# The sixth output pair's rows turned by VectorE instead of TensorE

## The chip, the cores and the metric

The kernel runs on one core of a Trainium2 chip. The time is the device time of one execution in microseconds (us), from start to end on that core. Profiles are of one execution, taken by the hardware profiler; in them PE is TensorE's matmul, PEld its weight load, DVE is VectorE, ACT ScalarE, POOL GpSimd and SP SyncE; a trailing q (SPq, ACTq) marks the queue that issues DMAs.

## The reference

One layer of masked attention over a graph of 2708 nodes with 1024 features, all in float32:

```python
h = jnp.maximum(_layernorm(x, axis=-1), 0.0)
q = h @ W_q.T + b_q;  k = h @ W_k.T + b_k;  v = h @ W_v.T + b_v
z = (1 / sqrt(1024)) * (q @ k.T)
spare_z = z * adj
spare_z = where(spare_z == 0.0, -10000.0, spare_z)
out = x + relu(softmax(spare_z, axis=1) @ v)
```

`adj` is 0 or 1 with a chance of 0.0014771 for a 1, so a row has about four neighbours.

## The kernel before

**What it computes.** Since rows have few neighbours, nothing dense of size 2708 x 2708 is formed. The kernel builds M = W_q^T W_k once, finds the neighbours of each row, sorts the rows by their number of neighbours and cuts them into tiles of 128 rows. For a tile t, K[t] is the largest number of neighbours in it. Sorted tiles with few neighbours have few slots: K is 3 for tile 18, 5 for 12, 2 for 19, 6 for 11, 4 for 15, 6 for 10, 4 for 14, 7 for 1, 4 for 16, 7 for 9 and 8 for 8. Then, for each tile:

- q = h M + b (a matmul with 1024 x 1024), stored to `q_dram` or `q_late`;
- **scores**: for each slot s, POOL gathers the neighbours' rows of h into a buffer `g` (L610, an indirect DMA), and one DVE instruction multiplies them with `pq`, the tile's q loaded back by SP (L833), and sums the products (L863);
- **weights**: an exponential on ACT, a few tiny DVE instructions (L906 to L911), and u = coef0 * g0 on ACT (L912);
- **sums**: for each further slot one DVE instruction u += coef * g (L923);
- out = x + relu(u W_v^T + b_v): another matmul with 1024 x 1024, then an indirect DMA that adds x (L1110) and one that scatters the rows (L808).

**Units.** Both matmuls are done for two tiles at a time, a *unit*, as a Strassen-Winograd product of 2 x 2 blocks with seven block products instead of eight. Units 0 to 9 form q (`q_pairs`), units 10 to 19 the output (`o_pairs`, in the order of `order`): 10 is (6, 5), 11 (4, 3), 12 (2, 0), 13 (20, 7), 14 (17, 13), 15 (18, 12), 16 (19, 11), 17 (15, 10), 18 (14, 1), 19 (16, 9). The sixth output pair is unit 15. Tile 8 is left over (`alone`) and done at the very end.

`multiply(n, results, after)` writes the seven products of unit n and calls `after(0)` to `after(6)` between them. In `after(i)` everything else is placed: `now` is [n, i], called step (n, i) here. The operands of unit n + 1 are made in unit n: `ops_of[n + 1][1]()` (upper) at i = 0 and `[2]()` (lower) at i = 2. Rows of unit n + 2 are loaded at i = 4 by `load_rows`.

**Turning.** A matmul needs the rows turned (features on partitions). `blocks(xa, xb)` has two ways for the rows of a tile:

- by TensorE: `half_turned` (L415) issues four 128 x 128 transposes for each half of a tile into PSUM. ACT copies three of a pair's four halves out (`held`, L718); DVE reads the fourth, a21, straight from PSUM for s1 and s3 (L722);
- by VectorE, for a tile that is *faced*: VectorE turns 32 x 32 blocks, so the blocks must already lie in the right partitions. When u is finished, ACT copies it into a tile `v` with its columns reordered (L945) and stores that (L947); `by_quarters` (L700) loads it back with four DMAs of 128 KB, each for 32 partitions, with 256 floats a piece; `faces` (L705) is one DVE transpose of 128 x 512 for each half. s3 is then formed in place (L742).

**Which way, and the generator.** All DVE work of the attention is one Python generator, `attention`, that yields a charge for each instruction: 1.3 for a score or a sum, 0.6 for weights. `advance(share)` in each `after` lets it go on until the charges reach `share`:

```python
share = (20.9 if n < len(units) - 5 else 21.5) / 7
if nxt is not None and nxt[0] == "o":
    share -= 2.3 / 7 * len(set(nxt[1:]) & faced_tiles)
```

so a unit that prepares a unit with faced tiles gets less of the stream. When the last sum of a tile t is issued, `sums(t)` decides by `now` and t's unit: faced (into `faced_tiles`); or, if `near(t)` (the unit is at most two ahead), *held*: u stays in its row buffer and becomes the rows of its unit without a store; or stored by SP (L951) and loaded by SP as a whole (L1212). Before the change, units 10 to 14 are faced, unit 19 and tile 8 too (`unit >= len(units) - 1`); of the others, 18, 12, 19 and 15 are stored and loaded, and 11, 10, 14 and 1 are held. If the tiles of unit n + 2 are not done when it loads, `advance(1.0)` is repeated until they are.

DVE runs in the order of the program (`manual_schedule`); the other engines' orders are the scheduler's. SP's queue also carries the loads of `pq` (two buffers), the store of one row for the tail (`tail_dram`, L1130) and its load (L1183). Row tiles (u, v and loaded rows) rotate through seven buffers. For tile 8, `faces` makes `T_alone` in unit 19, and the product `ps<-M,T_alone` uses it; after that come the last products and the final adds of x.

Of the kernel before, what the change touches and what calls it, by code (L numbers as in the profile page):

```python
# [65 lines left out]
def tile_preln_masked_attention(  # L66
# [144 lines left out]
    def row_tile(name):  # L211
        return work.tile([P, D], FT, tag="row", name=name, bufs=ROWS)
# [626 lines left out]
    def fill():  # L839
        while wanted and free:  # L840
            t, s = wanted.pop(0)
            g = free.pop(0)
            if s == K[t]:
                half = slice(HOSTS.index(t) * HP, (HOSTS.index(t) + 1) * HP)
                nc.gpsimd.dma_start(g[:HP], v_dram[half, :])
            else:
                with tc.issue_after(first_q[0].ins) if first_q else nullcontext():
                    gathered.append(gather(g, h_dram[:, :], t, s, P, skip=True))
            g_of[t].append(g)

    def chained(step):

        with tc.issue_after(chain[-1].ins):
            chain.append(step())
# [64 lines left out]
    def sums(t):  # L919
        u, coef, m = us.pop(t)  # L920
        for s in range(0 if t in EMPTY else 1, K[t]):
            fill()
            chained(lambda: nc.vector.scalar_tensor_tensor(  # L923
                u, g_of[t][s], coef[:, s:s + 1], u, op0=ALU.mult, op1=ALU.add))
            free.append(g_of[t][s])
            yield 1.3
        fill()
        if t in HOSTS:
            chained(lambda: nc.vector.scalar_tensor_tensor(
                u[:HP], g_of[t][K[t]][:HP], m[:HP, 3:4], u[:HP], op0=ALU.mult, op1=ALU.add))  # L930
            free.append(g_of[t][K[t]])
            yield 1.3
            fill()
        g_of.pop(t)
        if t == SECOND:
            nc.sync.dma_start(v_dram, u)
            whole_second.append(True)
            return
        unit = next((n for n, pair in enumerate(units) if pair[0] == "o" and t in pair[1:]), len(units))
        if now < [unit - 2, 2] and unit <= len(q_pairs) + 4 or unit >= len(units) - 1:  # L940
            faced_tiles.add(t)
        print("done", t, "at", now, "unit", unit, t in faced_tiles)
        if t in faced_tiles:
            v = row_tile(f"v_{t}")
            nc.scalar.copy(v.rearrange("p (a c r) -> p c a r", a=QUADS, r=QP),  # L945
                           u.rearrange("p (c a r) -> p c a r", a=QUADS, r=QP))
            nc.scalar.dma_start(u_dram[t * P:(t + 1) * P, :], v)  # L947
        elif near(t):
            held[t] = u
        else:  # L950
            nc.sync.dma_start(u_dram[t * P:(t + 1) * P, :], u)  # L951
        done.add(t)
# [7 lines left out]
    def attention(order):  # L960
        for t in order[:2]:
            ask(t)
        free.extend(slots)

        fetch(order[0])
        fill()
        yield 0.0
        marked(0, EARLY)
        yield 0.0
        after = order[1:] + [None, None]  # L970
        yield from scores(order[0], after[0])
        for i, t in enumerate(order):
            nxt = after[i]
            ahead = nxt is not None and K[t] + K[nxt] <= HIGH + 1
            part = scores(nxt, after[i + 1]) if nxt is not None else iter(())
            if ahead:

                for _ in range(min(2, K[nxt] - 1)):
                    yield next(part, 0.0)
            weights(t)  # L980
            yield 0.6
            if ahead:
                yield from part
            yield from sums(t)
            yield from part
# [8 lines left out]
    spent, now = [0.0], [0, 0]  # L994

    def near(t):

        return t == alone or any(t in unit[1:] for unit in units[:now[0] + 3] if unit[0] == "o")
# [193 lines left out]
    q_pairs = [(t, t + 1) for t in range(0, BARE, 2)]  # L1192
    o_pairs = [(order[i], order[i + 1]) for i in range(0, FULL - 1, 2)]
    alone = order[-1]
    units = [("q",) + p for p in q_pairs] + [("o",) + p for p in o_pairs]
# [367 lines left out]
```

## Time and profile before

| | |
|---|---|
| time, median of 3 runs | 638.43 us (636.95 to 638.96) |
| the profiled execution | 638.0 us, span 636.3 us |
| mean granted TensorE clock | 0.995 |
| busy: ACT, POOL | 283.5 us (45%), 361.8 us (57%) |
| moved by DMA | 180.11 MB, 283 GB/s on average |
| stores of faced tiles, `u_dram<-v` (ACT's queue) | 13 of 512 KB |
| loads by quarters, `or<-u_dram` | 52 of 128 KB |
| other stores and loads of u (SP) | 4 and 4 of 512 KB |

The span is from the first to the last instruction of the profile; the execution's own time is 1.7 us more. All times within the profile count from the start of the span. In the lines of groups and of the timeline, `out<-in` are the program's names, followed by the operand shapes and the count; what stands in brackets is the idle time of the engine just before and what ended it. In a timeline, equal neighbours are merged into one line with their count. The chain is the work that ended last, followed back from the last instruction.

### The profile page before, as it was taken

The numbers are of one execution on the slowest core, as the hardware profiler recorded it, in microseconds if no ns is written. First come the engines' busy times: TensorE is split into PE (matmuls) and PEld (weight loads), VectorE is DVE, ScalarE is ACT, GpSimd is POOL, SyncE is SP. The second block draws the span as 40 slices with busy tenths as digits, with TensorE's granted clock in tenths as the row PEclk, the third lists the DMA queues.
The fourth block names the chain that finished last, engine by engine and source line by source line (L and its number), as shares of the span: only waits on it lengthen the run. The fifth ranks groups of instructions, "written<-read, shape, count | busy, mean of one in ns | idle before, by whom it ended". The sixth has DMA issues, their size and how long they took to land.

```text
span 636.3 us, 6139 instructions
## 1 busy us (share of the span) xinstructions
PE 624.6 (98%) x1627; PEld 315.5 (50%) x1627; DVE 525.7 (83%) x1021; ACT 283.5 (45%) x421; POOL 361.8 (57%) x383
## 2 busy tenths in 40 slices
PE   9999999999999999999999999999999999999994
PEld 5777766444444544444444434444444444444441
DVE  5999889897995755997889999999999989898341
ACT  3539975859667533424341243443343333422300
POOL 2649960975868277563742563576566777632431
PEclk9999999999999999999999999999999999999997
DMA  8998897598696439986699998999999999893761
GB/s 339 407 372 310 334 351 298 199 342 328 246 382 221 170 113 334 326 299 196 194 289 323 297 412 216 311 318 324 351 378 321 334 299 295 242 289 95 210 217 40
DMA packets 62352, 180.11 MB, mean 283 GB/s; under 512 B 10039, under 2 KB 17031, under 8 KB 61672
## 3 DMA queue, kind: packets, MB, share of 16 engines
q0 software_dynamic: 25136, 78.41, 39.4%
q1 hardware_dynamic: 31242, 80.19, 35.8%
q10 hardware_dynamic: 5934, 21.06, 8.5%
q8 instruction: 15, 0.25, 0.2%
q14 instruction: 25, 0.20, 0.1%
HBM read 147.23 MB, written 42.31 MB: 298 GB/s over the span
## 4 chain that ended last, share of the span: by engine, by line
PE 85%; DVE 6%; issue 4%; DMA 3%; SPq 1%; POOL 0%; ACT 0%; POOLq 0%; DVEq 0%; ACTq 0%
PE ps L1011 38%; PE psy L1011 28%; PE ps_y L476 6%; PE ps_x L476 4%; PE ps_z L476 4%; PE pt L415 3%; DVE u L923 2%; DMA g<-h_dram,tab 1%; DMA or<-u_dram 1%; DVE junk L863 1%; DVE s L722 1%; DVE wlow L1270 1%; PE ps_y L511 1%; SPq L700 1%; DVE q L1092 0%
## 5 line engine op out<-in xcount | busy, mean ns | idle before, releaser
L610 POOL DMA_INDIRECT g<-h_dram,tab x94 | 121.4, 1291 | 84.4 <-DVE u L923 31.1
L1011 PE MATMUL ps<-M,a 128*128 128x512 f32 x320 | 144.0, 593 | 0.0
L1011 PE MATMUL psy<-wlow,s 128*128 128x512 f32 x320 | 143.9, 592 | 0.0
L863 DVE SCALAR_TENSOR_TENSOR junk<-g,pq 128x1024 uint8<-128x1024 f32 x93 | 113.7, 1222 | 14.0 <-DMA g<-h_dram,tab 10.9
L1011 PEld LDWEIGHTS ps<-M,a 128*128 128x128 f32 x320 | 59.8, 190 | 70.8 <-issue 70.6
L1011 PEld LDWEIGHTS psy<-wlow,s 128*128 128x128 f32 x320 | 59.7, 190 | 70.2 <-issue 69.4
L923 DVE SCALAR_TENSOR_TENSOR u<-g,coef,u 128x1024 f32<-128x1024 f32 x69 | 88.4, 1281 | 6.9 <-ACT u L912 5.8
L389 DVE FIND_INDEX8 at<-ones,adj 128x8 uint32<-128x685 f32 (+1 forms) x88 | 74.5, 865 | 0.0
L1011 PE MATMUL psy<-wlow,a 128*128 128x512 f32 x160 | 72.0, 593 | 1.4 <-DVE q L1092 1.4
L1011 PE MATMUL ps<-M,s 128*128 128x512 f32 x160 | 72.1, 592 | 0.0
L1011 PE MATMUL ps<-wlow,s 128*128 128x512 f32 x160 | 72.0, 593 | 0.1
L368 ACT ACTIVATE sized<-adj 128x2708 uint8<-128x2708 f32 (+1 forms) x22 | 54.3, 2468 | 7.5 <-DMA adj<-in_adj_dram 6.2
L298 POOL TENSOR_TENSOR hsum<-hsum,x 128x256 f32<-128x256 f32 (+1 forms) x56 | 38.7, 729 | 25.6 <-DVE wlow L444 21.2
L1110 POOL DMA_INDIRECT y<-in_x_dram,tab x19 | 34.8, 1832 | 29.1 <-ACT y L1127 15.9
L1011 PEld LDWEIGHTS psy<-wlow,a 128*128 128x128 f32 x160 | 30.3, 190 | 40.0 <-issue 37.1
L1011 PEld LDWEIGHTS ps<-wlow,s 128*128 128x128 f32 x160 | 30.3, 190 | 38.6 <-issue 37.9
L1011 PEld LDWEIGHTS ps<-M,s 128*128 128x128 f32 x160 | 30.3, 190 | 38.1 <-issue 37.4
L912 ACT ACTIVATE u<-g,coef 128x1024 f32<-128x1024 f32 x18 | 20.7, 1147 | 32.1 <-DVE coef L911 32.1
L808 POOL DMA_INDIRECT out_dram<-y,tab x21 | 25.0, 1188 | 16.4 <-DVE flag L1354 6.1
L626 POOL DMA_INDIRECT tab_dram<-tab,pos_i x22 | 21.9, 995 | 20.7 <-DVE pos_i L689 15.3
L276 ACT ACTIVATE x<-x,r 128x1024 f32<-128x1024 f32 (+1 forms) x22 | 25.9, 1235 | 7.3 <-POOL r L266 7.3
L760 ACT COPY ps<-bp_sb 128x512 f32<-128x512 f32 x42 | 24.5, 595 | 7.2 <-DVE y L1145 6.7
(251 smaller groups left out, 843.5 us busy)
## 6 DMA issues: line engine op xcount, KB each, us to landing
adj<-in_adj_dram SPq DMA_DIRECT2D x21, 1354.0 KB, 11.3
x<-in_x_dram SPq DMA_DIRECT2D x21, 512.0 KB, 3.9
h_dram<-x ACTq DMA_DIRECT2D x21, 512.0 KB, 8.7
u_dram<-v ACTq DMA_DIRECT2D x13, 512.0 KB, 6.4
or<-u_dram SPq DMA_DIRECT2D x52, 128.0 KB, 7.0
q_late<-q SPq DMA_DIRECT2D x12, 512.0 KB, 6.0
pq<-q_late SPq DMA_DIRECT2D x12, 512.0 KB, 8.6
M<-in_wv_dram SPq DMA_DIRECT2D x4, 1024.0 KB
```

The costliest lines, as they stand in the source:

```text
L276: nc.scalar.activation(xs[i][:n], xs[i][:n], AF.Relu, bias=r[:n, 4, i:i + 1], scale=r[:n, 3, i:i + 1])
L298: small.append(nc.gpsimd.tensor_add(hsum[:n, cols], hsum[:n, cols], xt[:n, cols]))
L368: nc.scalar.activation(sized[:n], a[:n, :, :PW], AF.Abs, accum_out=total[:n, t:t + 1])
L389: nc.vector.max_index(at[:n, k - first_k, g, :], ones[:n, 0:8], a[:n, g, :])
L476: mm = nc.tensor.matmul(bank, a_tile(o + H * a[0], a[1], i), b(o), start=first and o == 0, stop=(o == H - 1), skip_group_check=True)
L610: return nc.gpsimd.indirect_dma_start(out=dst, out_offset=None, in_=src, in_offset=off, bounds_check=N - 1, oob_is_err=False)
L760: nc.scalar.copy(return_[h], row[:, h * NB:(h + 1) * NB])
L808: to = nc.gpsimd.indirect_dma_start(out=out, out_offset=bass.IndirectOffsetOnAxis(ap=ptab.bitcast(U32)[:n, t, SLOTS:SLOTS + 1], axis=0), i ...
L863: chained(lambda: nc.vector.scalar_tensor_tensor(junk, g_of[t][s], 1.0, tq[t], op0=ALU.mult, op1=ALU.mult, accum_out=zall[:, t, s:s + 1]))
L923: chained(lambda: nc.vector.scalar_tensor_tensor(u, g_of[t][s], coef[:, s:s + 1], u, op0=ALU.mult, op1=ALU.add))
L1011: mm = nc.tensor.matmul(bank, a[:, c, :], b[:, c, :], start=False, stop=(c == 3), skip_group_check=True)
L1110: return nc.gpsimd.indirect_dma_start(out=y[:n], out_offset=None, in_=x, in_offset=off, compute_op=ALU.add)
```

## The change

The bound on the units whose tiles are faced goes up by one:

```diff
         unit = next((n for n, pair in enumerate(units) if pair[0] == "o" and t in pair[1:]), len(units))
-        if now < [unit - 2, 2] and unit <= len(q_pairs) + 4 or unit >= len(units) - 1:
+        if now < [unit - 2, 2] and unit <= len(q_pairs) + 5 or unit >= len(units) - 1:
             faced_tiles.add(t)
```

`len(q_pairs)` is 10, so unit 15, tiles 18 and 12, comes under the rule, if each of them is done before step (13, 2). For a faced tile the rest follows from code that is unchanged: ACT copies u to v and stores it, SP loads it by quarters, DVE turns it, and the share of the stream in unit 14 is reduced.

## The prediction

> **What bounds the kernel now.** I read the page first, its busy shares and its chain:
>
> ```profile
> PE 624.6 (98%) x1627; PEld 315.5 (50%) x1627; DVE 525.7 (83%) x1021; ACT 283.5 (45%) x421; POOL 361.8 (57%) x383
> DVE  5999889897995755997889999999999989898341
> PE 85%; DVE 6%; issue 4%; DMA 3%; SPq 1%; POOL 0%; ACT 0%; POOLq 0%; DVEq 0%; ACTq 0%
> ```
>
> PE is busy for 98% of the span, and VectorE (DVE) is nearly full just before the end. Next, the chain in order of time (start, length, what), where the two groups of transposes of unit 15 stand, and three lines of PE's timeline (start, busy time, instruction, count), the products that need s1 of unit 15 and T_alone among them:
>
> ```profile
> 468.94 0.87 PE pt L415 x8
> ...
> 473.25 0.87 PE pt L415 x8
> ```
> ```profile
> 487.70 3.60 PE L1011 MATMUL ps<-wlow,s 128*128 128x512 f32 x8
> ...
> 494.57 1.04 PE L415 MATMUL pt<-ident,or 128*128 128x128 f32 x8
> ...
> 609.69 3.60 PE L1011 MATMUL ps<-M,T_alone 128*128 128x512 f32 x8
> ```
>
> The chain runs through PE alone in the output stages up to the last few us, and PE's lines show no idle time there, so the end moves exactly as PE's instruction list does, until something on another engine makes PE wait. Two things can do that: the operands s1 to s4 of a pair, and T_alone, the turned rows of tile 8, for which the whole DVE stream must be over. The second is the tight one, in DVE's timeline:
>
> ```profile
> 468.41 2.61 DVE L923 SCALAR_TENSOR_TENSOR u<-M,coef,u 128x1024 f32<-128x1024 f32 x2
> 470.94 1.24 DVE L863 SCALAR_TENSOR_TENSOR junk<-g,pq 128x1024 uint8<-128x1024 f32 x1
> ...
> 591.14 1.27 DVE L929 SCALAR_TENSOR_TENSOR u<-g,m,u 64x1024 f32<-64x1024 f32 x1
> ...
> 605.03 1.25 DVE L705 STREAM_TRANSPOSE T_alone<-or 128x1024 f32<-128x1024 f32 x1 [11.56 <-DMA or<-u_dram]
> ```
>
> The stream ends at 591.14 + 1.27 = 592.41. A copy, a store and four loads later T_alone is made, ready at 606.28. PE needs it at 609.69. That is 3.41 us of cover today.
>
> **Does the edit act?** The charges of the generator (1.3 a score or sum, 0.6 a weight step, against the share of each step) give tile 18 finished at step (12, 2) and tile 12 at (12, 6). Both lie before (13, 2) and belong to unit 15 = 10 + 5, so both become faced. Nothing before them changes. In unit 14 the share falls by 2 x 2.3/7 a step, from 2.99 to 2.33, 4.6 in the seven steps. By the same charges tile 15 then ends at (15, 0) instead of (14, 5) and is held, not stored and reloaded; tile 1 would be late, and three or four stream steps are forced at (16, 4), which brings the lag back; tile 8 is recorded as done at (18, 6) instead of (18, 5).
>
> **PE.** Sixteen transposes of unit 15 go, two groups of eight at 0.87 each in the chain: 2 x 0.87 = 1.74 us, all on the path. This is also the most that the change can bring.
>
> **ACT.** Three copies out of PSUM go; two copies u to v (1.05 us each) and two store issues come, at about 430 and 443, when u_18 and u_12 are done. They fall into idle time:
>
> ```profile
> 435.88 1.15 ACT L912 ACTIVATE u<-g,coef 128x1024 f32<-128x1024 f32 x1 [5.34 <-DVE coef L911]
> ...
> 446.21 1.15 ACT L912 ACTIVATE u<-g,coef 128x1024 f32<-128x1024 f32 x1 [4.11 <-DVE coef L911]
> ...
> 592.44 1.05 ACT L945 COPY v<-u 128x1024 f32<-128x1024 f32 x1 [0.55 <-DVE u L929]
> ```
>
> Cost nothing; without the idle time it would be 2.1 us on an engine that is 45% busy.
>
> **DVE's work.** Four transposes of 128x512 come. The sums s1 and s3 read SBUF instead of PSUM (0.69 against 0.64 each: 0.1 together). Unit 14 shows the price, and how a lower half waits for its loads:
>
> ```profile
> 447.23 1.30 DVE L705 STREAM_TRANSPOSE a<-or 128x512 f32<-128x512 f32 x2
> 448.45 1.18 DVE L863 SCALAR_TENSOR_TENSOR junk<-g,pq 128x1024 uint8<-128x1024 f32 x1
> ...
> 452.68 0.71 DVE L705 STREAM_TRANSPOSE a<-or 128x512 f32<-128x512 f32 x1 [0.49 <-DMA or<-u_dram]
> 453.31 0.67 DVE L705 STREAM_TRANSPOSE s<-or 128x512 f32<-128x512 f32 x1
> 454.09 0.69 DVE L722 TENSOR_TENSOR s<-a,s 128x512 f32<-128x512 f32 x1
> ```
>
> From start to next start that is 1.22 + 1.41 = 2.63, with the sums 2.7 us. DVE's idle time in the stretch that matters is in brackets here (the line at 488.11 is the first score of tile 14, for later), and the queue's answer has the landing time of a gather:
>
> ```profile
> 476.19 1.28 DVE L722 TENSOR_TENSOR s<-a,pt 128x512 f32<-128x512 f32 x2 [1.04 <-ACT a L718]
> 480.77 1.23 DVE L863 SCALAR_TENSOR_TENSOR junk<-g,pq 128x1024 uint8<-128x1024 f32 x1 [0.82 <-DMA g<-h_dram,tab]
> 488.11 1.22 DVE L863 SCALAR_TENSOR_TENSOR junk<-g,pq 128x1024 uint8<-128x1024 f32 x1
> 500.99 1.23 DVE L863 SCALAR_TENSOR_TENSOR junk<-g,pq 128x1024 uint8<-128x1024 f32 x1 [0.96 <-DMA g<-h_dram,tab]
> 510.87 0.69 DVE L1122 TENSOR_TENSOR p<-taken,p 128x512 f32<-128x512 f32 x1 [0.28 <-ACT taken L1076]
> 523.78 1.22 DVE L863 SCALAR_TENSOR_TENSOR junk<-M,pq 128x1024 uint8<-128x1024 f32 x1 [1.83 <-DMA M<-h_dram,tab]
> ```
> ```profile
> g<-h_dram,tab POOLq DMA_INDIRECT x94, 7.8
> ```
>
> The 1.04 goes, since it waited for an ACT copy that no longer exists: net 2.7 - 1.04 = 1.66. The other four, 3.89 together, wait for transfers and for PE; a DVE that runs late finds these ready, as long as the gathers do not move with it. Bounds for what they give back: 0 and 3.89. I take all 3.89, because a gather is on its way 7.8 us (median) before it is used, and a DVE that runs some us late meets it landed.
>
> **The new wait.** DVE must now wait for quarter loads of u_18 and u_12. SP, the tile's landing times in unit 14 (430 to 445) and the store just ahead of unit 15's loads (445 to 460):
>
> ```profile
> 430.49 7.86 SPq L700 DMA_DIRECT2D or<-u_dram  x8
> ...
> 460.85 0.80 SPq L1212 DMA_DIRECT2D or<-u_dram  x2
> 464.56 0.32 SPq L833 DMA_DIRECT2D pq<-q_late  x1
> 464.93 0.36 SPq L1183 DMA_DIRECT2D y<-tail_dram  x1
> 465.35 0.41 SPq L1212 DMA_DIRECT2D or<-u_dram  x1
> ```
> ```profile
> L951 SPq DMA_DIRECT2D u_dram<-u x2: 320/329/338, 430.1 to 443.2; - x2
> DMA to landing us min/median/max: 7.9/13.0/14.5
> ```
> ```profile
> L951 SPq DMA_DIRECT2D u_dram<-u x1: 320/320/320, 458.1 to 458.1; - x1
> DMA to landing us min/median/max: 6.6/6.6/6.6
> ```
> ```profile
> 430.00:438.00 8.00, 8.00 (x20) 3.54 (x19) 7.76 (x17) 2.64 (x5) 3.68 (x3) 1.00 1.04 349
> 461.00:467.00 6.00, 6.00 (x15) 2.66 (x14) 5.86 (x11) 2.65 (x5) 2.60 (x2) 1.00 1.03 414
> ```
>
> In unit 14 the store ahead landed at 430.1 + 7.9 = 438.0 and the last quarter 14.5 later, at 452.5, as DVE's wait up to 452.68 says. The DMA engines were full (share 1.04), as they are at 461 to 467 (1.03). For unit 15 the store of u_19 is ahead and lands at 458.1 + 6.6 = 464.7, so the last quarter is due at 464.7 + 14.5 = 479.2. DVE reaches the upper half after the first of the two sums at 468.41, at 469.72. With its two transposes (1.22) and one sum and two scores (3.8) it would be at the lower half at 474.7. It loses 479.2 - 474.7 = 4.5 us, part of it already at the upper half, since the first tile's quarters are due halfway, at about 472. Bounds: nothing, if they land as in unit 12 (rival two), and 8.5 (rival one). Behind these waits in DVE's queue stand the scores of tile 10 and the results of unit 14; PE needs s1 of unit 15 at 487.70 - 1.74 = 485.96 and gets it at 479.2 + 1.41 + 0.69 = 481.3, so no PE wait here. On SP the loads of pq_14, of the tail rows and of tile 19 stand behind the quarters; the first is wanted by the score at 488.11, the last by PE's transposes at 494.57. The nearest has 8.8 us after the last quarter, so that costs nothing. The two copies v take two more of the seven row buffers for some us, as they do in the units before, and I cost that at nothing; if a buffer comes late, the quarters do, which is rival one.
>
> [...]
>
> **Sum.** The end of the stream moves by 1.66 + 4.5 - 3.89 = 2.27 (its later waits for ACT, after a weight step, stay as they are). The round trip from there to T_alone stays: copy, store, loads. PE comes 1.74 earlier, so the cover is 609.69 - 1.74 - 606.28 = 1.67, and PE waits 2.27 - 1.67 = 0.6. The profiled execution took 638.0: 638.0 - 1.74 + 0.6 = 636.9. That execution lies 0.43 below the median of the runs, 638.43, so the forecast is 637.3.
>
> **Rivals.**
>
> One, slower: the quarters come so late that DVE hands its delay to PE at T_alone. The place is the lower half of unit 15. If the eight issues are drawn out as in unit 14 (7.86 from 460.85, to 468.7) and the last lands 14.5 after that, at 483.2, DVE loses 8.5, the stream ends 6.3 late, PE waits 4.6: 640.9, or 641.3 on the median. It decides from a last landing of 480.3 on (PE's wait is then 1.74); each us more costs one. Gathers that move with DVE, so that the 3.89 is not given back, work the same way. For it: loads that are issued 9 us before they are wanted, where unit 14 had 17 and still waited. Against it: less traffic ahead than in unit 14, and tile 15 saves 1 MB later on.
>
> Two, the cover holds: the quarters land as those of unit 12, for which the tile's answer between 372 and 400 has this:
>
> ```profile
> L700 SPq DMA_DIRECT2D or<-u_dram x8: 303/394/432, 388.1 to 392.6; - x8
> DMA to landing us min/median/max: 4.8/5.1/5.4
> ```
>
> Then DVE hardly waits, its 1.66 vanishes in the idle time, and the whole 1.74 stays: 636.3, 636.7 on the median. Against it: the DMA engines are full at 461.
>
> Three, the edit does nothing because a tile is done too late: 638.4. The room of three steps from (12, 6) to (13, 2), in code that the change leaves alone up to there, speaks against it.
>
> **Numbers.** Forecast 0.39, rival one 0.31, two 0.27, three 0.03. The runs before spread from 636.95 to 638.96, 0.3%; that is about what a measurement of this kernel can tell from no change, 1.9 us. The largest gain, 1.74, is just under it: half of rival two and a third of the forecast would measure as faster (0.27), all of rival one as slower (0.31), the rest as the same (0.42). The range goes from 635.9 (rival two less 0.8 of spread) to 641.3 (rival one's price); what lies outside is gathers that move along.
>
> **What would show it.** Sixteen transposes fewer at L415 and four more at L705; or<-u_dram by quarters 60 times, whole once; u_dram<-u once. Right, if DVE's wait for or<-u_dram in unit 15 is 3 to 6 us and PE's only new wait is under 1.5 us, at T_alone. Wrong, if PE waits at s1 of any pair, if DVE's later waits for gathers stay at 3.89, or if T_alone is ready before 607.9 or after 610.

## The result and the profile after

The change is slower, by half a percent: 641.85 us median (637.24 to 643.71) against 638.18 us (636.95 to 640.85) for the kernel before on the same chip, a ratio of 1.0051, 95% interval 1.004 to 1.0062. The forecast was 637.3 us, at most 641.3. Of the 22 executions of the change, five took 637.24 to 639.24 us and seventeen 640.75 to 643.71. The profiled one took 643.71 us (span 642.0), the longest, so the sizes below are those of a bad run; a milder one comes with the experiments. The ratios below compare with the kernel before on each experiment's own chip, since chips differ (its medians there lie between 637.8 and 639.9).

The two lines of the page, busy shares and chain:

```profile
PE 623.2 (97%) x1611; PEld 313.4 (49%) x1611; DVE 528.1 (82%) x1025; ACT 283.1 (44%) x420; POOL 364.6 (57%) x383
PE 58%; issue 13%; DMA 13%; DVE 9%; POOL 5%; ACT 1%; POOLq 0%; DVEq 0%; SPq 0%; ACTq 0%
```

PE has 16 instructions fewer and DVE four more, as the edit says. But the chain, 85% PE before, now leaves PE for long stretches. PE's timeline (start, busy time, what, and in brackets the idle time ahead and its releaser) has three waits between 425 us and the end, where the kernel before had none:

```profile
493.51 3.70 PE L1011 MATMUL psy<-wlow,a 128*128 128x512 f32 x8 [3.04 <-ACT taken L1076]
614.10 3.70 PE L1011 MATMUL ps<-M,T_alone 128*128 128x512 f32 x8 [1.77 <-DVE T_alone L705]
618.45 3.70 PE L1011 MATMUL psy<-wlow,a 128*128 128x512 f32 x8 [0.65 <-DVE p L1151]
```

DVE's timeline, the waits and the end of the stream:

```profile
477.59 1.30 DVE L705 STREAM_TRANSPOSE a<-or 128x512 f32<-128x512 f32 x2 [6.58 <-DMA pq<-q_late]
...
484.54 0.71 DVE L705 STREAM_TRANSPOSE a<-or 128x512 f32<-128x512 f32 x1 [2.07 <-DMA or<-u_dram]
...
491.63 0.69 DVE L1126 TENSOR_TENSOR u<-ps,u 128x512 f32<-128x512 f32 x1
...
531.59 1.23 DVE L863 SCALAR_TENSOR_TENSOR junk<-g,pq 128x1024 uint8<-128x1024 f32 x1 [1.00 <-DMA g<-h_dram,tab]
...
560.44 2.61 DVE L923 SCALAR_TENSOR_TENSOR u<-g,coef,u 128x1024 f32<-128x1024 f32 x2 [1.61 <-ACT u L912]
...
585.08 3.92 DVE L923 SCALAR_TENSOR_TENSOR u<-g,coef,u 128x1024 f32<-128x1024 f32 x3 [1.22 <-ACT u L912]
...
599.21 1.28 DVE L929 SCALAR_TENSOR_TENSOR u<-g,m,u 64x1024 f32<-64x1024 f32 x1
...
612.80 1.25 DVE L705 STREAM_TRANSPOSE T_alone<-or 128x1024 f32<-128x1024 f32 x1 [11.25 <-DMA or<-u_dram]
```

The third wait of PE follows from the second: DVE makes that `p` behind T_alone. The two waits of DVE in unit 14 for the loads by quarters come to 6.58 + 2.07 = 8.65 us. (The first row names `pq` as the releaser, but the instruction reads only `or`, and SP issued the load of `pq` behind the quarters; a releaser in brackets is an inference.) SP, and the tile's landing times:

```profile
459.44 0.32 SPq L951 DMA_DIRECT2D u_dram<-u  x1
461.85 0.25 SPq L1130 DMA_DIRECT2D tail_dram<-y  x1
462.17 4.87 SPq L700 DMA_DIRECT2D or<-u_dram  x8
469.68 0.34 SPq L833 DMA_DIRECT2D pq<-q_late  x1
```
```profile
L700 SPq DMA_DIRECT2D or<-u_dram x8: 303/430/577, 462.2 to 466.6; - x8
...
DMA to landing us min/median/max: 12.2/15.1/16.7
```

What joins DVE's wait to PE's first one is ACT, whose rows come in the order of its list:

```profile
489.34 1.15 ACT L912 ACTIVATE u<-g,coef 128x1024 f32<-128x1024 f32 x1 [7.54 <-DVE coef L911]
492.35 0.63 ACT L1127 ACTIVATE y<-u 128x512 f32<-128x512 f32 x1 [1.86 <-DVE u L1126]
492.89 0.57 ACT L1076 COPY taken<-psy 128x512 f32<-128x512 f32 x1
```

The copy `taken` empties the PSUM bank that PE adds a22 of unit 14 to next. It needs nothing from DVE. But in ACT's list it stands behind a weight step (489.34) and behind `y<-u`, which waits for DVE's add at 491.63, and both come late because in DVE's list their sources stand behind the loads by quarters. So the wait for unit 15's rows stops a product of unit 14.

The account fits. Without its waits PE would reach T_alone at 614.10 - 1.77 - 3.04 = 609.29; the forecast had 609.69 - 1.74 = 607.95. So this run is 1.34 us late beside its bracketed waits. PE is 0.92 of that late ahead of the edit's place (the product that started at 465.35 before starts at 466.27), and the rest is that the waits delay PE's next starts by 0.2 to 0.3 us more than their brackets say. DVE is 1.32 us late at that place (the sums that started at 464.45 before start at 465.77). The stream ends at 599.21 + 1.28 = 600.49, that is 600.49 - 592.41 - 1.32 = 6.76 us later than before. DVE's idle stretches of over 0.15 us from 460 us to the stream's end sum to 8.72 us before (the prediction's 4.93, and 1.62, 0.95 and 1.22 behind them); in this run 4.11 of such idle is left beside the 8.65 (the three bracketed rows behind 484.54, and 0.28). With 2.7 us of added work: 2.7 + 8.65 - (8.72 - 4.11) = 6.74.

### The profile page after: what moved, and what is told of

Its sections match the earlier page's. It is cut to its first block, busy times and chain, and to the rows that moved or that the text cites. A ratio compares the mean times of both kernels' runs of the same rounds, so it can differ in the third digit from the quotient of the medians.

```text
span 642.0 us, 6113 instructions
## 1 busy us (share of the span) xinstructions
PE 623.2 (97%) x1611; PEld 313.4 (49%) x1611; DVE 528.1 (82%) x1025; ACT 283.1 (44%) x420; POOL 364.6 (57%) x383
## 4 chain that ended last, share of the span: by engine, by line
PE 58%; issue 13%; DMA 13%; DVE 9%; POOL 5%; ACT 1%; POOLq 0%; DVEq 0%; SPq 0%; ACTq 0%
PE ps L1011 23%; PE psy L1011 17%; PE ps_y L476 6%; PE ps_x L476 4%; PE ps_z L476 4%; PE pt L415 3%; DMA out_dram<-y,tab 3%; POOL g L610 3%; DMA M<-h_dram,tab 3%; DVE u L923 3%; DVE junk L863 2%; DMA or<-u_dram 2%; DMA g<-h_dram,tab 1%; DMA v_dram<-u 1%; DVE s L722 1%
## 5 line engine op out<-in xcount | busy, mean ns | idle before, releaser
L1110 POOL DMA_INDIRECT y<-in_x_dram,tab x19 | 33.4, 1758 | 29.2 <-ACT y L1127 21.2
L808 POOL DMA_INDIRECT out_dram<-y,tab x21 | 27.7, 1319 | 11.6 <-issue 5.2
L945 ACT COPY v<-u 128x1024 f32<-128x1024 f32 x15 | 15.7, 1045 | 33.4 <-DVE u L923 28.3
```

The lines of the kernel that those rows point to most:

```text
L808: to = nc.gpsimd.indirect_dma_start(out=out, out_offset=bass.IndirectOffsetOnAxis(ap=ptab.bitcast(U32)[:n, t, SLOTS:SLOTS + 1], axis=0), i ...
L1110: return nc.gpsimd.indirect_dma_start(out=y[:n], out_offset=None, in_=x, in_offset=off, compute_op=ALU.add)
```

## The experiments

Each kernel is the change with one edit more, unless it says otherwise. In the code only the lines that matter are shown, and `...` marks what is left out.

**Loads earlier, loads whole, the share, one tile.** The first question was whether the late quarters are the cause (L) or DVE's added work and the smaller share of the stream (W).

e1_early:

```diff
-                if i == (2 if n in (FIRST, last_q) else 4) and n + 2 > FIRST ...
+                if i == (2 if n in (FIRST, last_q) else 0 if n == 13 else 4) and n + 2 > FIRST ...
```

> The changed kernel, with unit 15's quarter loads written at step (13, 0) instead of (13, 4), so that SP issues them ahead of the store of u_19 and of the tail row. Theory L (the quarters land too late; the changed kernel's DVE waited 6.6 and 2.1 us for them in unit 14): the two waits fall to under 1 us, PE's 3.0 us wait behind ACT's copy and its 1.8 us wait for T_alone go, and the time falls by 4 to 5 us, to 636.5 to 637.5, a little under the kernel before. Theory W (2.7 us more DVE work and fewer stream steps in unit 14 are too much by themselves): the waits of unit 14 go, but PE still waits 2 to 5 us at T_alone, and the time stays at 640 to 642.

Measured: 1.0116 (1.0102 to 1.0131), a miss. SP's timeline, DVE's and PE's show why:

```profile
427.33 25.70 SPq L700 DMA_DIRECT2D or<-u_dram  x16
453.95 0.34 SPq L833 DMA_DIRECT2D pq<-q_late  x1
```
```profile
469.09 1.22 DVE L863 SCALAR_TENSOR_TENSOR junk<-g,pq 128x1024 uint8<-128x1024 f32 x1 [11.65 <-DMA pq<-q_late]
```
```profile
472.13 5.40 PE L1011 MATMUL psy<-wlow,s 128*128 128x512 f32 x8 [3.89 <-ACT psy L1024]
```

The quarters were there in time, but sixteen of them keep SP's queue busy for 25.7 us, and DVE waits 11.65 us for q of tile 15, which stands behind them. So the earlier load is no remedy here: the next tile's q waits in the same queue.

e2_whole:

```diff
-                if t in faced_tiles:
+                if t in (18, 12):
+                    faced.append(rows[-1])
+                    nc.sync.dma_start(rows[-1], u_dram[t * P:(t + 1) * P, :])
+                elif t in faced_tiles:
```

> The changed kernel, but tiles 18 and 12 are loaded whole, one DMA of 512 KB with 4 KB rows each, at the same place; the transposes of DVE stay. The rows then lie in the wrong order for these two tiles, so their output is not the reference's; all work is there. Theory L: the loads land within 8 us or so, as the whole loads of the kernel before did (needed by PE at 468.8 after an issue at 460.9), DVE waits under 2 us, and the time is 636.5 to 637.5. Theory W: 640 to 642, with PE waiting at T_alone.

Measured: 0.9981 (0.9972 to 0.999). DVE's timeline has the same transposes, with no brackets:

```profile
470.70 1.30 DVE L705 STREAM_TRANSPOSE a<-or 128x512 f32<-128x512 f32 x2
...
475.52 0.70 DVE L705 STREAM_TRANSPOSE a<-or 128x512 f32<-128x512 f32 x1
```

DVE's added work and the smaller share are all there, PE's 16 transposes are gone, the loads are whole, and the kernel gains. This refutes W.

e3_share, and e4_one:

```diff
-        if nxt is not None and nxt[0] == "o":
+        if nxt is not None and nxt[0] == "o" and n != 14:
```
```diff
-        if now < [unit - 2, 2] and unit <= len(q_pairs) + 5 or unit >= len(units) - 1:
+        if now < [unit - 2, 2] and (unit <= len(q_pairs) + 4 or t == 18) or unit >= len(units) - 1:
```

> The changed kernel with the share of unit 14 left at 2.99 as before (the cut of 2 x 2.3/7 a step left out for this unit), so the order of stream steps is that of the kernel before and tile 15 is stored and loaded again. Theory L: the quarters are as late as ever, DVE waits 8 to 9 us in unit 14, and more stream steps stand between the waits and PE's needs: 641.5 to 645. Theory W in the form that the planner's cut does the harm: back to 637 to 638.5.

> Only tile 18 is turned by DVE; tile 12 is stored, loaded whole and turned by PE as before. PE saves 0.87 us instead of 1.74, DVE has 1.3 us more work instead of 2.7. Theory L: four quarters land in half the time after the store of u_19, DVE waits 2 to 5 us at the upper half and hardly at the lower, and the kernel comes out within 1 us of the kernel before, 637.5 to 639.5. Theory W: halfway, 639.5 to 640.5.

Measured: 1.0072 (1.0058 to 1.0086) and 1.0095 (1.0073 to 1.0118). In the first, DVE still waits 6.66 us for the quarters and PE 3.37 us for `taken`; it does not wait for T_alone. So the share moves the place of the loss, not its cause. The second, with half the quarters, is slower than either of its theories had (640.5 us at most, against 644.82 measured), because PE itself waits:

```profile
477.90 1.94 PE L415 MATMUL pt<-ident,or 128*128 128x128 f32 x8 [5.07 <-DMA or<-u_dram]
```

Tile 12's whole load was issued at 462.51, behind four quarters, and PE's wait for it ends 15.4 us later.

**What makes a load by quarters slow.** It differs from a whole load in two ways: pieces of 1 KB, and 32 partitions for each DMA. Four combinations tell them apart. f1_rows4 and its repeat h2_rows4 load 32 whole rows in each of four DMAs; h1_pieces loads one quarter of the columns to all partitions in each of four; h3_whole repeats e2_whole:

```diff
+                    for a in range(QUADS):
+                        part = slice(a * QP, (a + 1) * QP)
+                        nc.sync.dma_start(rows[-1][part], u_dram[t * P:(t + 1) * P, :][part])
```
```diff
+                    for g in range(QUADS):
+                        part = slice(g * 256, (g + 1) * 256)
+                        nc.sync.dma_start(rows[-1][:, part], u_dram[t * P:(t + 1) * P, part])
```

> The loads of tiles 18 and 12 stay four DMAs of 32 partitions each, but each brings 32 whole rows of 4 KB instead of pieces of 1 KB; the rows of these two tiles then come out in another column order, so part of the output is other numbers. Loads whole gave 636.96 us and no wait of VectorE. Theory P (the pieces of 1 KB are what is slow beside the gathers' 4 KB): the quarters land within some 8 us of their issue, VectorE's wait in unit 14 is under 1.5 us, PE does not wait, 636.5 to 637.4. Rival theory Q (the cut into four DMAs of 32 partitions, eight issues on SP instead of two, is what is slow): VectorE still waits 6 to 9 us and the time is 640.5 to 642.

> Tiles 18 and 12 are loaded by four DMAs each, as in the change, but each DMA brings one quarter of the columns to all 128 partitions: pieces of 1 KB stay, the cut by 32 partitions goes. The rows of these tiles then lie in another order, so part of the output is other numbers. If the pieces of 1 KB are what is slow: VectorE's waits for these loads stay at 4 us or more, DMA moves under 270 GB/s while they are served, ratio 1.003 or more. If the 32 partitions are what is slow: VectorE waits under 1.5 us, DMA moves over 330 GB/s there, as with whole loads, ratio 0.997 to 1.000.

> A repeat of the loads in four DMAs of 32 whole rows of 4 KB, beside the others on one chip. Expected as before: VectorE's wait for the quarters about 1 us, later waits for gathers 5 to 6 us, about 250 GB/s while the quarters are served, PE waits about 2 us for T_alone, ratio 1.000 to 1.003. If the 32 partitions are not what is slow, it should now be like whole loads, 0.998.

> A repeat of the whole loads (one DMA for each tile, rows of 4 KB, 128 partitions), beside the others on one chip: no wait of VectorE for them, over 340 GB/s while they are served, PE does not wait at T_alone, ratio 0.997 to 0.999.

The windows from 467 to 473 us, a stretch right behind the issue of these loads (busy time of PE, PEld, DVE, ACT and POOL, then granted clock, DMA share, GB/s), of the change, h3_whole, h1_pieces and h2_rows4:

```profile
467.00:473.00 6.00, 6.00 (x15) 2.66 (x14) 3.91 (x4) 2.91 (x6) 5.08 (x4) 1.00 1.10 226
```
```profile
467.00:473.00 6.00, 6.00 (x16) 2.65 (x15) 5.89 (x7) 2.74 (x6) 4.64 (x4) 1.00 1.05 397
```
```profile
467.00:473.00 6.00, 6.00 (x16) 2.65 (x15) 5.45 (x7) 1.50 (x3) 5.08 (x4) 1.00 1.05 310
```
```profile
467.00:473.00 6.00, 6.00 (x15) 2.50 (x14) 4.79 (x6) 2.81 (x6) 4.86 (x4) 1.00 1.05 227
```

The DMA share is full in all four; what the full engines move is not the same.

| loads of tiles 18 and 12 | GB/s | DVE waits for them | PE waits at T_alone | ratio |
|---|---|---|---|---|
| rows of 4 KB, 128 partitions (e2, h3) | 382, 397 | 0, 0 | 0, 0 | 0.9981 (0.9972 to 0.999), 0.9988 (0.9974 to 1.0002) |
| pieces of 1 KB, 128 partitions (h1) | 310 | 0.44 | 0 | 1.0002 (0.9982 to 1.0021) |
| rows of 4 KB, 32 partitions (f1, h2) | 251, 227 | 0.91, 1.14 | 2.10, 0.98 | 1.0012 (0.9996 to 1.0028), 1.0008 (0.9994 to 1.0023) |
| pieces of 1 KB, 32 partitions (the change, and f3_order below) | 226; with the same loads 222 in h4_late1 and 215 in g1_late, both below | 8.65, 5.12 | 1.77, 0.50 | 1.0051 (1.004 to 1.0062), 1.0055 (1.0033 to 1.0078) |

The waits come from one execution each. For whole loads, for rows to 32 partitions and for the change there is a longer execution and a shorter one among the two. For h1_pieces there is only the shortest of twelve (637.60 us): five of these took up to 639.49 us and seven 640.76 to 642.90, and what DVE waits for in those seven was not seen.

In these executions either one alone makes DVE wait at most 1.14 us for the quarters; both together cost 5 to 9. What slows the traffic is above all the 32 partitions: with them it is 215 to 251 GB/s whatever the piece, without them 310 (pieces; between the two bounds of its expectation) or 382 and 397 (rows). Over the longer stretch from 461 to 485 us the gap is smaller: the means of its four windows of 6 us are 314 to 320 GB/s with 32 partitions (h2_rows4, the change, f1_rows4, h4_late1) and 354 to 366 without (h1_pieces, h3_whole, e2_whole). DVE waits longer for the gathers too. Its later waits in h2_rows4:

```profile
485.40 1.23 DVE L863 SCALAR_TENSOR_TENSOR junk<-g,pq 128x1024 uint8<-128x1024 f32 x1 [1.10 <-DMA g<-h_dram,tab]
...
514.04 1.23 DVE L863 SCALAR_TENSOR_TENSOR junk<-g,pq 128x1024 uint8<-128x1024 f32 x1 [1.39 <-DMA g<-h_dram,tab]
528.23 1.23 DVE L863 SCALAR_TENSOR_TENSOR junk<-g,pq 128x1024 uint8<-128x1024 f32 x1 [2.33 <-DMA g<-h_dram,tab]
```

These are 4.82 us together (5.75 in f1_rows4). The kernel before had 3.61 of such waits with a DVE that came earlier; h1_pieces, with a late one, has none. All of DVE's idle time from 460 us to the stream's end, 8.72 us before, is 6.50 to 7.69 in e2_whole, h1_pieces and h3_whole, 9.87 and 10.58 in h2_rows4 and f1_rows4, 9.16 in f3_order and 12.76 in the change. So f1_rows4 lies between its two theories: DVE's wait for the quarters is as short as P said, but PE waits for T_alone, and the traffic is slow. The ratios of the middle rows overlap; the bytes and the waits, not the times, separate them. Why 32 partitions go with slow traffic, no run here shows.

**Where DVE stands when it waits.** g1_late turns unit 15's halves two steps later, h4_late1 one step later:

```diff
-                if i == (3 if n == 0 else 4 if turn else 0):
+                if i == (3 if n == 0 else 4 if turn else 2 if n == 14 else 0):
...
-                if i == (4 if n == 0 else 5 if turn else 2):
+                if i == (4 if n == 0 else 5 if turn else 4 if n == 14 else 2):
```

> Only the place of unit 15's turning in VectorE's list is changed: the upper half is turned at step 2 of unit 14 instead of step 0 and the lower half at step 4 instead of step 2, each about 7 us later; the loads stay as they are. Theory (the loss is VectorE standing in its queue for loads by quarters that are on their way): by then the quarters are there, VectorE's waits for them are under 3 us in place of 8.65, the copy taken and T_alone are not late, s1 of unit 15 comes close to when PE wants it; ratio to the kernel before 0.997 to 1.000 in place of 1.005. Rival (the traffic or the work itself is too much, wherever the wait stands): VectorE's time is lost elsewhere, or PE waits 2 us or more for s1, ratio 1.003 or more.

> The change, with the turning of unit 15 one step later in VectorE's list: upper half at step 1, lower half at step 3 of unit 14 (two steps later gave 1.0033, with waits for gathers in place of the waits for quarters). If the slower traffic is what costs, wherever the wait stands: VectorE's waits from unit 14 on stay about 2 us above those of the kernel before, ratio 1.002 to 1.005. If it was s1 coming late: PE has no wait at s1, and the ratio is 0.998 to 1.001.

Measured: 1.0033 (1.0013 to 1.0053) and 1.0036 (1.0018 to 1.0054). DVE and PE in g1_late:

```profile
483.05 1.22 DVE L863 SCALAR_TENSOR_TENSOR junk<-g,pq 128x1024 uint8<-128x1024 f32 x1 [3.50 <-DMA g<-h_dram,tab]
...
528.46 1.23 DVE L863 SCALAR_TENSOR_TENSOR junk<-g,pq 128x1024 uint8<-128x1024 f32 x1 [2.97 <-DMA g<-h_dram,tab]
```
```profile
486.37 3.67 PE L1011 MATMUL ps<-wlow,s 128*128 128x512 f32 x8 [0.76 <-DVE s L722]
610.37 3.70 PE L1011 MATMUL ps<-M,T_alone 128*128 128x512 f32 x8 [1.60 <-DVE T_alone L705]
```

The wait for the quarters and PE's wait for `taken` are gone, but DVE now waits for gathers, and PE waits nearly as long for T_alone as in the change. DVE's idle time from 460 us to the stream's end is 10.74 us, 2.0 more than before; with 2.7 us of work the stream ends 4.9 us later (597.32 against 592.41). That is the second cost that goes with the slow traffic (215 GB/s from 467 to 473 us): DVE's waits for gathers are 6.64 us here (3.50, 0.17 and 2.97) against 3.61 before. The wait that ends at 483.05 is for the gather of the fifth score of tile 10; before, POOL issued it at 469.59 and the wait for it ended at 480.77, 2.3 us earlier. When POOL issued it in g1_late, no row here shows. h4_late1 shows less of this: its waits for gathers are 3.86 us against 3.61 before, and its whole idle time from 460 us on is 8.79 us against 8.72, where about 2 more was expected. So what brings its 1.08 us at T_alone is mainly DVE's 2.7 us of work, for which nothing is given back and of which the cover takes 1.67. Its trace is of a shorter execution (640.08 us, median 642.92).

**ACT's order.** f3_order wrote unit 14's `y<-u` behind `taken` in the program; g2_order also held it there:

```diff
+            if late:
+                with tc.issue_after(copy.ins):
+                    nc.scalar.activation(ya[:, hi], late.pop(), AF.Relu)
```

> The changed kernel, but in unit 14 ACT's relu of the product's first lower block (y<-u) is issued behind the copy taken instead of ahead of it, so ACT does not stand on a result of VectorE before it gives PE the copy. Theory: PE's wait of 3.04 us before psy<-wlow,a at 493 goes; VectorE is as late as before (waits of 6 to 9 us in unit 14), so the wait at T_alone grows by the part that the first wait had covered, up to 1.77 + 3.04: between 638.8 (the 3.04 is gained) and 641.8 (it only moves to T_alone). Rival: the first PE wait is not due to ACT's order, it stays at about 3 us, 641.5 to 642.

> The changed kernel, but in unit 14 ACT's relu y<-u is now held behind the copy taken (the first try left them in their old order). The weight step u<-g,coef of tile 1 still stands ahead of the copy. Theory: PE's wait before psy<-wlow,a (3.04 in the profile of the change) falls to 1 us or less; what it gave VectorE as time comes back at T_alone in part, where the wait may grow from 1.77 up to 4: ratio 1.002 to 1.005. Rival: VectorE's lateness alone decides, whatever ACT does, and the ratio stays at 1.005 to 1.006.

(The weight step that g2_order's expectation gives to tile 1 is tile 15's.) In f3_order the scheduler kept the old order on ACT (`y<-u` at 489.09, `taken` at 489.63), so it is a second sample of the change, and a telling one: ratio 1.0055 (1.0033 to 1.0078), with a profiled execution of 639.68 us, the fastest of its runs.

```profile
473.79 1.31 DVE L705 STREAM_TRANSPOSE a<-or 128x512 f32<-128x512 f32 x2 [2.51 <-DMA or<-u_dram]
...
481.28 0.71 DVE L705 STREAM_TRANSPOSE a<-or 128x512 f32<-128x512 f32 x1 [2.61 <-DMA or<-u_dram]
```
```profile
610.26 3.70 PE L1011 MATMUL ps<-M,T_alone 128*128 128x512 f32 x8 [0.50 <-DVE T_alone L705]
```

The quarters cost 5.12 us here, PE does not wait for `taken`, and T_alone costs 0.50: nearly the forecast's numbers. What differs most between the two executions is when the quarters land. In g2_order the order did change (`taken` at 484.95, `y<-u` at 486.90), and the ratio is 1.0045 (1.003 to 1.0059), not to be told from the change's. Its profiled run had quarters as early as f3_order's (DVE waits 4.67 us for them), where PE would not have waited for `taken` anyway. So the chain by way of ACT is seen in the change's trace, and in e3_share's; what its removal gives in the median run stays open: the two ratios differ by 0.0006, less than their intervals can tell, and no longer execution of g2_order has a trace.

**Other ways to load.** g3_two_queues sends tile 12's quarters on ACT's queue; g4_mid issues both tiles' at step (13, 2).

```diff
-                    by_quarters(rows[-1], u_dram[t * P:(t + 1) * P, :])
+                    by_quarters(rows[-1], u_dram[t * P:(t + 1) * P, :], nc.scalar if t == 12 else None)
```
```diff
-                if i == (2 if n in (FIRST, last_q) else 4) and n + 2 > FIRST ...
+                if i == (2 if n in (FIRST, last_q, 13) else 4) and n + 2 > FIRST ...
```

> The quarter loads of tile 12 are issued by ACT on its own queue, those of tile 18 stay with SP. Theory P (pieces of 1 KB on one queue get a small share beside the gathers): two queues get about twice the share, the last quarter lands some 5 us earlier, VectorE waits under 4 us in place of 8.65, ratio 0.999 to 1.002. Rival (the DMA engines as a whole are full, and a second queue only shares the same): VectorE waits 7 us or more, ratio 1.004 or more.

> Unit 15's quarter loads are issued at step 2 of unit 13 instead of step 4, about 7 us earlier; issued at step 0 they blocked the load of q of tile 14 in SP's queue. Theory: the quarters land some 5 us earlier, VectorE's wait in unit 14 is under 4 us; whether q comes late decides the rest: with q on time 0.999 to 1.002, with q late as in the run at step 0 1.006 or more. Rival: unit 14's quarters and unit 15's are then in SP's queue together and land no earlier, VectorE waits 7 us or more as before.

Measured: 1.0054 (1.0033 to 1.0074) and 1.0105 (1.0085 to 1.0126). With two queues DVE waits 7.86 us, all of it at the upper half, as the rival had it (7 us or more); that full DMA engines are the reason was not shown. At (13, 2) DVE waits 11.80 us for q of tile 15 (the expectation has it as tile 14's), as in e1_early.

f2_scat moves the cut into the store (ACT stores in pieces to the places where a whole load wants them), for tiles 18 and 12; f4_scat6 does so for all faced tiles but 8, and takes unit 16 under the rule too:

```diff
-            nc.scalar.dma_start(u_dram[t * P:(t + 1) * P, :], v)
+                to = u_dram[t * P:(t + 1) * P, :].rearrange("(a r) (g j) -> g r a j", a=QUADS, g=QUADS)
+                for g in range(QUADS):
+                    nc.scalar.dma_start(to[g], v[g * QP:(g + 1) * QP, :].rearrange("r (a j) -> r a j", a=QUADS))
```

> For tiles 18 and 12 the rearrangement into 32-partition blocks moves from the load to the store: the store on ACT's queue is four DMAs that write pieces of 1 KB, and SP loads each tile whole in rows of 4 KB. Theory P: the small pieces are then in the store, which lies some 15 us ahead of the load, VectorE's wait in unit 14 is under 1.5 us, 636.5 to 637.4 (0.998 of the kernel before). Rival: pieces of 1 KB are slow in the store as well, the loads wait for the store and issue late, VectorE waits 4 us or more and the time is 639 or more.

> The rearrangement is moved into the store for every tile that VectorE turns except tile 8, and unit 16 (tiles 19 and 11) is turned by VectorE too. PE does 32 transposes of 128x128 fewer than the kernel before, 2 x 1.74 = 3.5 us. If VectorE keeps up (2.7 us more for each unit, covered by its waits for gathers and the cover at T_alone of 3.4): 634.9 to 635.5. If VectorE is what is short, the second pair's 2.7 us come out at T_alone and the time is 636.5 to 638.

Measured: 1.0055 (1.0033 to 1.0077) and 1.0186 (1.0168 to 1.0205). ACT in f2_scat:

```profile
445.97 7.85 ACTq L950 DMA_DIRECT2D u_dram<-v  x3
453.87 1.15 ACT L912 ACTIVATE u<-g,coef 128x1024 f32<-128x1024 f32 x1 [7.30 <-DMA u_dram<-v]
```

The store is now what is cut by 32 partitions, and three of its issues hold ACT for 7.85 us. DVE waits for unit 14's quarters instead, 5.28 us and then 2.73. So the cost went one unit forward, and what the cut in the store alone costs is not shown. f4_scat6 missed both its theories (638 us at most, 651.23 measured): PE waits 2.80 us at 396.63 and 3.31 at 407.08 already, and 3.40 at T_alone; the rest was not traced.

i1_all128 spreads 32 rows of u_dram over all 128 partitions with each DMA, so that the rows lie as VectorE needs them without the 32 partitions, for all faced tiles; i2_all128_before does it without the edit:

```diff
-                              rows[:, cols].rearrange("(g r) j -> r g j", r=QP))
+            nc.sync.dma_start(dst[:, g * 256:(g + 1) * 256],
+                              rows[g * QP:(g + 1) * QP, :].rearrange("r (a j) -> a r j", a=QUADS))
```

> The change, with every load by quarters cut the other way: four DMAs for a tile, each taking 32 rows of u_dram and spreading their four pieces of 1 KB over all 128 partitions, in one quarter of the columns. The rows come out exactly as before. If the 32 partitions of a DMA were what is slow: VectorE waits under 1 us for these loads in units 13 to 15, DMA moves over 290 GB/s between 467 and 473 us, PE has no wait at the copy taken nor at T_alone, and the 1.74 us of PE are gained: ratio 0.996 to 0.999. If other things made it slow (the pieces in DRAM lie 1 KB apart in rows of 4 KB, which is the same here): VectorE waits 3 us or more, ratio 1.002 or more.

> The kernel before, without the edit, with the same loads over all 128 partitions for its faced tiles. PE has no wait in the output stages of the kernel before, so faster loads have nothing to give there: ratio 0.999 to 1.001, and the edit is worth the difference to the run beside it, about 0.0027 if it gains its whole 1.74 us. Rival: the loads themselves save time elsewhere, and this kernel gains as much as the one with the edit.

Measured: 1.1262 (1.1246 to 1.1278) and 1.0933 (1.0909 to 1.0957), misses by far. SP in i1_all128:

```profile
452.41 33.35 SPq L699 DMA_DIRECT2D or<-u_dram  x8
```

Eight issues take 33.35 us, where the change's eight take 4.87, while the DMA share falls to 0.53 between 461 and 467, at 197 GB/s: here the 16 engines together are not full, and the loads are slow even so. In i2_all128_before the share is 0.40 between 467 and 473, at 150 GB/s. Why, no run here shows. As an experiment on the 32 partitions i1_all128 decides nothing, since its loads are slow with engines that are not full, and whether the edit gains with fast loads of the rows as VectorE needs them stays open. The only kernels ahead of the one before (e2_whole, and h3_whole, whose interval just includes 1) load the rows in another order.

## Why the prediction was wrong, point by point

- **The edit acts; PE saves 1.74; ACT's copies are free; DVE has 2.7 us more work.** These held: the counts, the account above, and e2_whole, where with fast loads the ratio is 0.9981, 1.2 us of the 1.74.
- **The step that failed is the wait for the quarters: 4.5 us forecast, 8.65 us in the profiled run.** The landing was taken as one number, 14.5 us behind the store, from one load in one execution of the kernel before. That number was also misread: in its view it is the time from a quarter's own issue to its landing, which fits the store's landing too only because the last quarter was issued just then (438.0). In the change's trace the eight issues go from 462.2 to 466.6, and the view has 12.2 to 16.7 us to landing. In that run's own time, less DVE's 1.32, DVE is released at 484.54 - 1.32 = 483.2, just rival one's landing, where the forecast had 479.2. In f3_order, taken the same way (its DVE is 1.60 us late at the same place), it is 479.7; in g2_order (0.16 early) 479.2. So the forecast described an early run. The landing moves over some 4 us (479.2 to 483.2) from run to run. That the long executions, 17 of the change's 22, are those with late quarters is argued from these traces (643.71 us late, 639.68 and 639.15 early); why it varies stays open.
- **What is given back: 4.93 with the 1.04, measured 4.61.** Right for this run. But it was argued from gathers that land long before DVE comes. In g1_late and h2_rows4, beside the slow traffic (215 and 227 GB/s), DVE waits 6.64 and 4.82 us for them, so the give-back holds only where DVE has lost the time already.
- **"No PE wait here" was wrong in what it looked at.** It asked only for s1 of unit 15, and for that it was right, though not by the 4.7 us that it had: s1 is ready at 485.95 + 0.69 = 486.64, and PE's product starts at 486.87. It listed the results of unit 14 as standing behind the waits in DVE's queue, but did not follow them on: DVE's add, ACT's `y<-u`, ACT's `taken` behind it, PE. That is 3.04 us.
- **The wait at T_alone: 0.6 forecast, 1.77 measured.** With the measured 6.74 in place of 2.27 and a round trip to T_alone 0.31 us shorter, PE would have waited 6.74 - 0.31 - 1.67 = 4.8; the 3.04 that it had lost already leave 1.7. Each us that PE loses earlier is cover here.
- **Rival one had the right mechanism and size (8.5 us, 641.3), but the wrong place:** it put all the loss at T_alone. That its 8.5 is so close is in part luck: it had the eight issues drawn out over 7.86 us and the usual time to landing, where they took 4.87 and the landing took longer; and it had DVE wait at the lower half, where 6.58 of the 8.65 are at the upper. What lay above its price is that the losses ahead of T_alone are not bounded by it: 3.04 + 1.77 + 0.65 = 5.46 us in place of 4.6.
- **The quarters' shape.** The forecast took their landing over from unit 14 as it stood there. h1_pieces, with pieces of 1 KB alone, has the rows nearly in time in the one execution seen (0.44 us); the 32 partitions are what goes with the slow traffic (215 to 251 GB/s), and sending half of the quarters on a second queue leaves DVE's wait at 7.86 us.

## What to carry to other kernels

Price a transfer by its shape as well as its bytes: for 6 us a load cut by partitions took a full set of DMA engines (share 1.05 to 1.14) from some 390 to between 215 and 251 GB/s, and in four runs (h4_late1, h2_rows4, f1_rows4, g1_late) DVE's waits for gathers were 3.86 to 6.64 us, against 3.61 before. When an engine gets a new wait, follow each instruction behind it to the other engines' lists until you reach the bound engine; the first victim here was a copy that needed nothing from the waiting engine (3.04 us of PE). And when a cover is a few us, ask how much a landing time varies from run to run (here some 4 us) before taking it from one row.

## What was not expected of the hardware

- A full DMA share did not tell the bytes: at 1.05 to 1.14 the stretch from 467 to 473 us moved from 215 to 397 GB/s, by the shape of one tile pair's loads.
- DVE waited longer for the gathers beside the loads to 32 partitions: 4.82 (h2_rows4) and 5.75 us (f1_rows4) with rows of 4 KB, not at all with pieces of 1 KB to 128 (with whole loads 1.92 and 0.66).
- In i1_all128 the order of one dimension in the loads cost more than all else: 33.35 us for eight issues of 128 KB, with a DMA share of 0.53.
